# Statistics behind the next maxima, a router's sum one slot later, and an aggregation behind an eviction in a fused attention and routing kernel

## Chip, cores and metric

The kernel runs on one core of one Trainium2 chip. The metric is the device time of one execution in microseconds (us). TensorE multiplies matrices into PSUM, VectorE and ScalarE read PSUM and SBUF, GpSimd reads SBUF, and SyncE issues most of the transfers. In the profile these are PE (with PEld for the loads of weights), DVE, ACT, POOL and SP.

## The reference

The input `x` has 8 batches of 512 rows and 2048 columns. First comes attention in windows of 128 columns with 8 heads, its queries and keys from the normalised `x`, its values from a context. Then each row picks 8 of 64 experts from its normalised logits, is scaled by the sum of their weights and gets a mixture of their biases.

```python
q   = einsum('ed,bdw->bew', Wq, qp) + bq      # qp: patches of layernorm(x)
k   = einsum('ed,bdw->bew', Wk, qp) + bk
val = einsum('ed,bdw->bew', Wv, vp) + bv      # vp: patches of the context
attn = softmax(where(mask > 0, q·k / sqrt(32), -1e9))
o    = gelu(attn · val)
x    = x + tanh(g_xattn) * (Wo·o + bo) * masks
flat   = layernorm(x)                         # over the 2048 columns
scores = softmax(flat @ router_weight.T + router_bias)
topk_w, topk_idx = top_k(scores, 8)
out = x + tanh(g_ffn) * (flat * topk_w.sum() + w_dense @ expert_bias)
```

Two layer norms need the mean and variance of whole rows of 2048 columns: one of `x` ahead of the attention of a batch, one of the attention's result ahead of the batch's routing.

## The kernel before

**Slots.** Each batch is cut into 4 chunks of 512 columns and each chunk into 2 halves of two windows. One half is one slot, g = 0 to 63. A loop runs slots 0 to 61 (8 for a batch, the number called `SPB`); the last two are written out behind it. The order of instructions on every engine is that of the program, by hand; each engine, and SyncE's queue of transfers, takes its instructions strictly in that order.

**A slot on TensorE:** the scores of g (L418) into four PSUM tiles `sc0` to `sc3`, the weighing of values of g-2 (L494), in even slots two output products of chunk ch-2 (`attend`, L524) and in odd ones its logits (L559), the turning of g-1's weights (L472), half of the next chunk's queries and keys (`queries_and_keys`, L356), turnings of the attention's result (`turn_x`, L548), the values of the next chunk's half (L393), and in odd slots two more output products. Values use the tile `sc0`, so the next slot's scores wait until VectorE has evicted the values (`values_out`, L402, tile `vT`). The products of queries and keys, the output products and the logits share two PSUM buffers with the tag `mm` in turn, so each waits for VectorE to read the product before the last. Queries and keys take seven products per half of the features, in four buffers; the fifth product needs the buffer that the sum in L364 reads last.

**A slot on VectorE:** the maxima of g (16 instructions, L437), in even slots two evictions of output products (L530) and the mask (L295), in odd slots the eviction of the logits (L575, L577), the reciprocal of the first sums of exponentials (L457, which needs ScalarE's exponentials, L449), the copies and sums of queries and keys (L363 to L383), the second reciprocal, statistics, the eviction of values, and in odd slots two evictions of output products.

**Statistics of x** come in pieces of 512 columns: 16 for a batch, each loaded (`load_raw`, L91, two buffers) and read by one `bn_stats` (`stats_x`, L245); reading a piece also issues the load of the piece two further on, on SyncE's queue, where it waits for the read. Batch 1 is read in slots 0 to 4, 2, 2, 4, 4 and 4 pieces, later batches two per slot. `stats()` reads the first `PER` = 2 of a slot behind the queries and keys; the call `read_x(len(pieces))` at the slot's end reads what is left, which is two pieces in slots 2, 3 and 4 and none elsewhere. In slot 5 (and every eighth from there) `aggregate` joins the statistics of the next batch.

**Statistics of the result** (`statistics2`, L543) are joined for a batch by `aggregate` in slots with `fin == 2`: slots 10, 18, ... 58. It has four `bn_aggr` on VectorE (L228) and seven small instructions on GpSimd (L230 to L236); their results are read in the next slot by `choose`.

**The router's weights** are centred once: `router_sums` adds them up over the contraction (L772, VectorE), and `centre_router` at the end of slot 3 makes the mean on TensorE (L777) and subtracts it on VectorE (L778). The first logits are those of slot 5.

Of the kernel before, what the change touches and what calls it, by code (L numbers as in the profile page):

```python
# [22 lines left out]
def flamingo_gated_kernel(  # L23
# [34 lines left out]
    NCH = S // CW  # L58
# [35 lines left out]
    def load_xn(ch):  # L94
        t = work.tile([P, NM, CW], F32, tag="xn", name=f"xn_{ch}")
        nc.sync.dma_start(t, rows_of(x, ch // NCH, columns(ch)))
        xn[ch] = t
# [115 lines left out]
    st1, ln1, st2, lns, nmrs = {}, {}, {}, {}, {}  # L213
# [78 lines left out]
    def mask(ch):  # L292

        m01s[ch] = work.tile([P, CW], F32, tag="m01", name=f"m01_{ch}")
        nc.vector.tensor_scalar(m01s[ch], mks[ch], 0.0, scale, ALU.is_gt, ALU.mult)  # L295
# [102 lines left out]
    def values_out(ch, h):  # L398
        pv = pvs.pop((ch, h))
        del cxs[ch, h]  # L400
        vT = work.tile([P, NPP, DK], F32, tag="vT", name=f"vT_{ch}_{h}", bufs=4)
        nc.vector.tensor_tensor(vT, pv, bv_sb[:, None, :].to_broadcast([P, NPP, DK]), ALU.add)  # L402
        vTs[ch, h] = vT
# [74 lines left out]
    def turned(g, k, engine=nc.scalar):  # L478
        p = pairs[g]
        i, e = k // NE, k % NE  # L480
        copy(engine, p["atT"][i][:, e * HR : (e + 1) * HR, :], p.pop("pt"))
# [87 lines left out]
    def logits_out(ch, ms=slice(0, NM)):  # L569
        b = ch // NCH  # L570
        ds = slice(ms.start * P, ms.stop * P)
        pl = pls.pop(ch)[:, ds]
        if ch % NCH == 0:
            lgT[b] = work.tile([P, D], F32, tag="lgT", name=f"lgT_{b}", bufs=1)
            nc.vector.tensor_copy(lgT[b], pl)  # L575
        else:
            nc.vector.tensor_tensor(lgT[b][:, ds], pl, lgT[b][:, ds], ALU.add)  # L577


    experts = {}  # L580
# [190 lines left out]
    def router_sums():  # L771
        nc.vector.tensor_reduce(rwsum, rw_sb.rearrange("p k e -> p e k"), AX.X, ALU.add)  # L772
# [11 lines left out]
    PER = NPIECE // SPB  # L784
    last = NC - 1
    pieces_left = [(b, i) for b in range(1, B) for i in range(NPIECE)]
    for g in range(NG - NH):
        ch, h = g // NH, g % NH
        even = h == 0
        nxt = ch + 1  # L790

        g1 = g - 1 if g >= 1 else None
        g2 = g - 2 if g >= 2 else None

        n_pieces = [2, 2, 4, 4, 4][g] if g < 5 else PER
        pieces = [pieces_left.pop(0) for _ in range(n_pieces) if pieces_left]

        mb, mk = (g - LAG) // SPB, (g - LAG) % SPB
        steps = [mk] if mb >= 0 else []
        xch = ch - 2 if even and ch >= 2 else None  # L800
        lch = ch - 2 if not even and ch >= 2 else None
        pch = ch - 1 if not even and ch >= 1 else None

        vals = [] if (nxt, h) in ((1, 0), (last, NH - 1)) else [(nxt, h)]
        b4 = ch // NCH - 1
        fin = g % SPB if b4 >= 0 else None

        def turn_(k):
            if g1 is not None:
                turn(g1, k)  # L810
                turned(g1, k)

        def turn_x_(k):
            if xch is not None:
                turn_x(xch, k)


        if even:
            if nxt > 1:
                load_cx(nxt, 1)  # L820
            if nxt < last and nxt + 1 >= NCH:
                load_xn(nxt + 1)
        elif nxt < last:
            load_cx(nxt + 1, 0)
        if even and NCH <= ch - 1:
            load_xr(ch - 1)


        scores(g)
        if g2 is not None:  # L830
            weigh(g2)
            weighed(g2)
        maxima(g, (0, 1))
        maxima(g, (2, 3))

        def read_x(n):

            for b, i in pieces[:n]:
                stats_x(b, i)
                if queue:  # L840
                    load_raw(*queue.pop(0))
            del pieces[:n]

        exps(g, 0)
        if even:
            if xch is not None:
                for m in (2, 3):
                    attend(xch, m)
                del os_[xch], mks[xch]
            exps(g, 1)  # L850
            exps(g, 2)
            if g > 0:
                mask(nxt)
            turn_(0)
            turn_(1)
            exps(g, 3)
            if fin != 4:
                for k in steps:
                    scale_x(mb, k)
            if g > 0:  # L860
                divide(g, 0)
            if g == 0:
                load_mask(2)
        else:
            exps(g, 1)
            if lch is not None:
                logits(lch)
                logits_out(lch)
            turn_(0)
            exps(g, 2)  # L870
            exps(g, 3)
            for k in steps:
                scale_x(mb, k)
            if g > 1:
                divide(g, 0)
            b1 = g // SPB + 1
            if g % SPB == 5 and b1 < B:
                ln1[b1] = aggregate(st1.pop(b1), S // 512, f"1_{b1}")
                shares_of_mean(b1)


        def between(i):
            if even:
                if g == 0 and i == 0:
                    divide(g, 0)
                    mask(nxt)
                turn_x_(i)
            elif i == 0:
                if g == 1:
                    divide(g, 0)  # L890
                turn_(1)
                if fin == 3:
                    gather_halves(b4)
                if pch is not None:
                    gelu(pch)
            else:
                turn_(2)
                if pch is not None and nxt < last:
                    load_mask(nxt + 1)

        if even:
            new_queries_and_keys(nxt)
        queries_and_keys(nxt, h, between)
        if not even:
            mask_bias(nxt)
        if fin == 3:
            add_halves(b4)
            choose(b4)
        divide(g, 1)
        if not even and nxt < last:  # L910

            if (nxt + 1) % NCH == 0:
                norm(nxt + 1)
            sums_of_x(nxt + 1, 0)


        if fin == 4:
            select(b4)
        def stats():

            sch = xch if fin != 4 else None
            if fin == 5:
                sch = ch - 2
            if sch is not None:
                for m in range(NM):
                    statistics2(sch, m)
            read_x(PER)

        if fin != 4:
            stats()  # L930
        if fin == 2:
            nmean, rs = aggregate(st2.pop(b4), NCH, f"2_{b4}")
            experts[b4] = {"nmean": nmean, "rs": rs}


        if even:
            turn_x_(2)
            for c_, h_ in vals:
                values(c_, h_, 0, 0)
                turn_(2)  # L940
                values(c_, h_, 1)
            if not vals:
                turn_(2)
            if nxt < last and (nxt + 1) % NCH:
                norm(nxt + 1, (0, 1))
            for c_, h_ in vals:
                values_out(c_, h_)
            if fin == 4:
                stats()
            if fin == 4:  # L950
                turn_weights(b4)
            turn_x_(3)
            turn_(3)
            if nxt < last and (nxt + 1) % NCH:
                norm(nxt + 1, (2, 3))
            if fin == 4:
                for k in steps:
                    scale_x(mb, k)
        else:
            turn_(3)  # L960
            if pch is not None:
                table_of_exps()
            if fin == 3:
                choose_exps(b4)
            for c_, h_ in vals:
                values(c_, h_, 0, 0 if g > 1 else None)
                values(c_, h_, 1)
                values_out(c_, h_)
            if pch is not None:

                for m in (0, 1):
                    attend(pch, m, r=m + 1 if steps else None)
            if nxt < last:
                sums_of_x(nxt + 1, 1)
                sums_of_x(nxt + 1, 2)
        if g == 1:
            nc.scalar.activation(wo_sb, wo_sb, AF.Copy, scale=tgates[:, 0:1])
        if g == 2:
            router_sums()
        if g == 3:  # L980
            centre_router()
        if g == 5:
            load_experts()
        read_x(len(pieces))
        for k in steps:
            mix(mb, k)

# [2 lines left out]
    g = h0 + 1  # L990
# [185 lines left out]
```

## Time and profile before

| | |
|---|---|
| median of three runs | 1316.97 us (1316.94 to 1317.23) |
| the profiled execution's own time | 1316.82 us |
| its span, first to last instruction | 1314.9 us |
| granted TensorE clock, mean | 0.997 |

The stretches from one slot's scores to the next one's, with the busy time of each engine in them (us):

| slot | from, to | length | PE | DVE | ACT | POOL |
|---|---|---|---|---|---|---|
| 2 | 58.00, 72.50 | 14.50 | 14.04 | 10.33 | 10.02 | 10.04 |
| 3 | 72.50, 90.78 | 18.28 | 17.38 | 13.13 | 14.27 | 7.37 |
| 4 | 90.78, 110.41 | 19.63 | 19.09 | 16.58 | 10.63 | 13.18 |
| 5 | 110.41, 130.66 | 20.25 | 19.09 | 12.43 | 15.99 | 9.63 |
| 6 | 130.66, 149.62 | 18.96 | 18.82 | 14.36 | 11.95 | 13.32 |
| 7 | 149.62, 168.43 | 18.81 | 18.81 | 10.96 | 14.48 | 7.25 |
| 10 | 206.21, 225.65 | 19.44 | 18.82 | 14.84 | 12.44 | 13.73 |
| 18 | 364.17, 383.98 | 19.81 | 19.81 | 14.92 | 12.80 | 15.01 |

The granted clock is 1.00 in all of them. From slot 12 on a step of the expert mixture of the batch before is added to each slot (L698 on TensorE, L716 on VectorE). A line of a timeline has the start, the duration, the engine, the line, the operation, the tile written and the tiles read, how many were merged, and in brackets the idle time of the engine before it with what ended it.

### The profile page before, as it was taken

The page shows a single profiled execution, that of the slowest core. Times are in us where ns is not written, and L with a number is a line of the kernel's source. Part 1 is how long each engine was busy: PE and PEld are TensorE (multiplying, and loading weights), DVE is VectorE, ACT ScalarE, POOL GpSimd, SP SyncE. Part 2 cuts the span into 40 slices and gives each one's busy share as a digit, 9 for nine tenths or more (in the row PEclk, how much of TensorE's full clock was granted, in tenths as well). Part 3 has the DMA queues.
Part 4 walks back from the last instruction along what each step waited for, and adds up shares of the span by engine and source line. Part 5 has one row for each costly group of instructions (what it writes and reads, how often), then busy time and mean ns, then how long its engine had stood idle before and what let it go on. Part 6 is the DMA issues. An engine that isn't in the chain of part 4 may idle for free. (4 is left out here: it accounts for less than half of the span.)

```text
span 1314.9 us, 27786 instructions
## 1 busy us (share of the span) xinstructions
PE 1292.9 (98%) x9536; PEld 944.4 (72%) x9536; DVE 925.9 (70%) x3613; ACT 870.1 (66%) x2838; POOL 791.6 (60%) x812
## 2 busy tenths in 40 slices
PE   9999999999999999999999999999999999999996
PEld 6777777777777777777777777777777777777653
DVE  4876767677677776777676786677776776666777
ACT  2776866676765775857667666667656767657652
POOL 3655556675566755577655667556666665575643
PEclk9999999999999999999999999999999999999999
DMA  8333434253444443453443453533544424423224
GB/s 285 97 105 113 114 105 137 97 165 93 152 153 134 149 137 105 152 169 127 155 119 124 153 165 119 167 99 128 169 145 137 153 65 129 138 98 104 73 73 176
DMA packets 109693, 173.40 MB, mean 132 GB/s; under 512 B 9200, under 2 KB 43632, under 8 KB 109424
## 3 DMA queue, kind: packets, MB, share of 16 engines
q1 hardware_dynamic: 107776, 169.27, 40.0%
q10 hardware_dynamic: 1776, 2.36, 0.5%
q8 instruction: 75, 1.23, 0.4%
q14 instruction: 66, 0.54, 0.1%
HBM read 138.06 MB, written 33.55 MB: 131 GB/s over the span
## 5 line engine op out<-in xcount | busy, mean ns | idle before, releaser
L458 POOL TENSOR_TENSOR at<-at,rsum 128x1024 f32<-128x1024 f32 x128 | 244.2, 1908 | 297.5 <-DVE rsum L457 279.8
L449 ACT ACTIVATE at<-at,nmx 128x128 f32<-128x128 f32 x1024 | 396.4, 392 | 4.9 <-DVE nmx L437 4.4
L393 PE MATMUL pv<-wv_sb,cx 128*128 128x256 f32 x1024 | 238.4, 381 | 2.1 <-DMA cx<-in_ctx 2.1
L524 PE MATMUL po<-o,wo_sb 128*128 128x512 f32 x512 | 234.0, 599 | 0.4 <-ACT o L518 0.4
L437 DVE CUSTOM_DVE_ANT_0 at<-sc,m 128x128 f32<-128x128 f32 x1024 | 220.7, 285 | 5.8 <-PE sc L418 5.8
L393 PEld LDWEIGHTS pv<-wv_sb,cx 128*128 128x128 f32 x1024 | 188.5, 191 | 24.7 <-DMA cx<-in_ctx 2.5
L533 POOL TENSOR_TENSOR xr<-t,xr 128x512 f32<-128x512 f32 x124 | 161.4, 1314 | 67.7 <-DVE t L530 67.7
L449 ACT ACTIVATION_READ_ACCUMULATOR at<-at,nmx 128x1 f32 x1024 | 195.0, 190 | 0.0
L476 ACT COPY o<-pa 128x512 f32<-128x512 f32 x63 | 36.9, 585 | 231.2 <-PE pa L494 231.2
L476 ACT COPY atT<-pt 128x512 f32<-128x512 f32 x254 | 140.6, 576 | 52.9 <-PE pt L472 52.7
L524 PEld LDWEIGHTS po<-o,wo_sb 128*128 128x128 f32 x512 | 94.3, 190 | 100.6 <-issue 84.1
L472 PEld LDWEIGHTS pt<-ident,at 128*128 128x128 f32 x1024 | 121.8, 141 | 56.6 <-issue 36.9
L472 PE MATMUL pt<-ident,at 128*128 128x128 f32 x1024 | 150.7, 275 | 0.7 <-ACT atT L476 0.3
L530 DVE SCALAR_TENSOR_TENSOR t<-po,bo_sb,mk 128x512 f32<-128x512 f32 x128 | 95.7, 749 | 62.3 <-PE po L524 62.3
L476 ACT COPY x1T<-px 128x512 f32<-128x512 f32 x120 | 70.2, 586 | 96.0 <-PE px L548 95.9
L356 PE MATMUL qk<-xt,wq_sb 128*128 128x256 f32 x496 | 128.0, 381 | 2.5 <-DVE u L364 2.5
L356 PE MATMUL qk<-xn,wk_sb 128*128 128x256 f32 x496 | 127.8, 380 | 1.6 <-DVE lgT L575 1.2
L356 PE MATMUL qk<-xn,ws 128*128 128x256 f32 x496 | 127.3, 379 | 0.0
L356 PEld LDWEIGHTS qk<-xn,ws 128*128 128x128 f32 x496 | 94.3, 190 | 12.8
L716 DVE TENSOR_TENSOR xr<-pb,xr 128x512 f32<-128x512 f32 x128 | 81.7, 684 | 30.1 <-PE pb L698 30.1
L356 PEld LDWEIGHTS qk<-xn,wk_sb 128*128 128x128 f32 x496 | 89.3, 190 | 11.9 <-DVE lgT L575 1.6
L418 PEld LDWEIGHTS sc<-ks,qs 32*128 32x128 f32 x2048 | 63.2, 186 | 45.8 <-DVE t L530 18.2
(118 smaller groups left out, 2070.3 us busy)
## 6 DMA issues: line engine op xcount, KB each, us to landing
out_dram<-xr SPq DMA_DIRECT2D x63, 512.0 KB, 3.6
cx<-in_ctx SPq DMA_DIRECT2D x62, 512.0 KB, 5.4
raw<-in_x SPq DMA_DIRECT2D x112, 256.0 KB, 3.4
xn<-in_x SPq DMA_DIRECT2D x28, 1024.0 KB, 7.6
xr<-in_x SPq DMA_DIRECT2D x28, 1024.0 KB, 7.5
mk<-in_mask_Bx1x_ff SPq DMA_DIRECT2D x32, 256.0 KB, 5.4
xr<-in_x SPq DMA_DIRECT2D x12, 256.0 KB, 6.3
cx<-in_ctx ACTq DMA_DIRECT2D x2, 512.0 KB, 6.6
```

The source lines that it names most:

```text
L356: nc.tensor.matmul(out_, w_[:, j, es], xb[:, j, :], start=(j == 0), stop=(j == NM // 2 - 1))
L393: nc.tensor.matmul(pv[:, i, :], cx[:, m, i * W : (i + 1) * W], wv_sb[:, m, :], start=(m == 0), stop=(m == NM - 1),)
L418: nc.tensor.matmul(sc[r][:, i, e, :], qss[ch][rows[r], e, ws], kss[ch][rows[r], e, ws], start=True, stop=True,)
L437: nc.vector.tensor_tensor_reduce(p["at"][i][:, e * HR + r, :], p["sc"][r][:, i, e, :], bias, -1.0, BIG, ALU.add, ALU.min, p["nmx"][:, r, i ...
L449: nc.scalar.activation(at, at, AF.Exp, bias=p["nmx"][:, r, i, e : e + 1], scale=-1.0, accum_out=p["rsum"][:, i, h : h + 1],)
L458: (engine or nc.gpsimd).tensor_tensor(p["at"][i], p["at"][i], rs[:, :, None].to_broadcast([P, H, W]), ALU.mult)
L472: nc.tensor.transpose(pt[:, r, :], p["at"][i][:, e * HR + r, :], ident)
L476: (engine.tensor_copy if engine is nc.vector else engine.copy)(out_, in_)
L524: nc.tensor.matmul(po[:, cs], wo_sb[:, e, m * P : (m + 1) * P], os_[ch][:, e, cs], start=(e == 0), stop=(e == NE - 1),)
L530: nc.vector.scalar_tensor_tensor(t[:, cs], po[:, cs], bo_sb[:, m : m + 1], mks[ch][:, cs], ALU.add, ALU.mult)
L533: (engine or nc.gpsimd).tensor_tensor(xc, t[:, cs], xc, ALU.add)
L716: nc.vector.tensor_tensor(xc, pt, xc, ALU.add)
```

## The change

Three moves of instructions within VectorE's order (the first with the loads that it issues on SyncE's queue, the last with the seven instructions on GpSimd); nothing else is changed.

- The pieces that slots 2, 3 and 4 leave over are read in the following slot (3, 4 and 5): in an even slot behind the maxima, the evictions of output products and the mask; in an odd slot behind the maxima and the eviction of the logits. The read at the slot's end is gone.
- `router_sums` goes from the end of slot 2 into slot 3, behind the statistics and ahead of the eviction of values.
- In slots with `fin == 2` the aggregation goes from ahead of the values to behind their eviction.

```diff
@@ -784,6 +784,7 @@
+    pieces = []
     for g in range(NG - NH):
@@ -793,6 +794,7 @@
         n_pieces = [2, 2, 4, 4, 4][g] if g < 5 else PER
+        over = pieces
         pieces = [pieces_left.pop(0) for _ in range(n_pieces) if pieces_left]
@@ -833,7 +835,7 @@
-        def read_x(n):
+        def read_x(n, pieces=pieces):
@@ -851,6 +853,7 @@
             if g > 0:
                 mask(nxt)
+            read_x(len(over), over)
             turn_(0)
@@ -866,6 +869,7 @@
                 logits(lch)
                 logits_out(lch)
+            read_x(len(over), over)
             turn_(0)
@@ -928,9 +932,8 @@
         if fin != 4:
             stats()
-        if fin == 2:
-            nmean, rs = aggregate(st2.pop(b4), NCH, f"2_{b4}")
-            experts[b4] = {"nmean": nmean, "rs": rs}
+        if g == 3:
+            router_sums()
@@ -945,6 +948,9 @@
             for c_, h_ in vals:
                 values_out(c_, h_)
+            if fin == 2:
+                nmean, rs = aggregate(st2.pop(b4), NCH, f"2_{b4}")
+                experts[b4] = {"nmean": nmean, "rs": rs}
             if fin == 4:
@@ -975,13 +981,10 @@
-        if g == 2:
-            router_sums()
         if g == 3:
             centre_router()
         if g == 5:
             load_experts()
-        read_x(len(pieces))
         for k in steps:
```

## The prediction

> **What bounds the kernel.** I read the page's first part, then TensorE's timeline from start to end, then VectorE's and ScalarE's timelines around each hole found there. The page:
>
> ```profile
> span 1314.9 us, 27786 instructions
> ...
> PE 1292.9 (98%) x9536; PEld 944.4 (72%) x9536; DVE 925.9 (70%) x3613; ACT 870.1 (66%) x2838; POOL 791.6 (60%) x812
> ```
>
> TensorE is busy for 98%, so a change of order on VectorE pays only where TensorE stands still for VectorE. The chain of waits covers only the last 15 us and tells nothing here. In TensorE's timeline between 36 and 1230 us seven matmul groups carry an idle time, all before 226 us; the change touches what precedes four of them:
>
> ```profile
> 80.06 1.13 PE L356 MATMUL qk<-xt,wq_sb 128*128 128x256 f32 x4 [0.90 <-DVE u L364]
> ...
> 97.88 1.13 PE L356 MATMUL qk<-xn,wk_sb 128*128 128x256 f32 x4 [0.41 <-DVE t L530]
> ...
> 117.94 1.13 PE L356 MATMUL qk<-xn,wk_sb 128*128 128x256 f32 x4 [1.16 <-DVE lgT L575]
> ...
> 225.65 1.17 PE L418 MATMUL sc<-ks,qs 32*128 32x128 f32 x32 [0.62 <-DVE vT L402]
> ```
>
> They lie in slots 3, 4, 5 and at the end of slot 10. The reader sees a start, a duration, and in brackets how long TensorE waited and for whom. From slot 12 (244.90) to slot 61 (1221.30) the starts of successive scores lie 19.80 to 20.32 us apart in a fixed pattern with no such wait, so a microsecond won before them is kept to the tail.
>
> What VectorE does ahead of those holes:
>
> ```profile
> 72.36 1.95 DVE L772 TENSOR_REDUCE rwsum<-rw_sb 128x64 f32<-128x1024 f32 x1
> 74.24 1.27 DVE L245 BATCH_NORM_STATS2 st<-raw 128x6 f32<-128x512 f32 x2
> 75.43 0.26 DVE L437 CUSTOM_DVE_ANT_0 at<-sc,m 128x128 f32<-128x128 f32 x1
> ...
> 112.61 1.31 DVE L245 BATCH_NORM_STATS2 st<-raw 128x6 f32<-128x512 f32 x2 [2.26 <-DMA raw<-in_x]
> 113.83 0.27 DVE L437 CUSTOM_DVE_ANT_0 at<-sc,m 128x128 f32<-128x128 f32 x1
> ...
> 224.43 0.61 DVE L228 BATCH_NORM_AGGREGATE mv<-st 128x2 f32<-128x24 f32 x4
> 224.96 0.63 DVE L402 TENSOR_TENSOR vT<-pv,bv_sb 128x512 f32<-128x512 f32 x1
> ```
>
> The router's sum and two pieces stand between slot 2's values and slot 3's maxima, two pieces (with a wait for their load) before slot 5's maxima, the aggregation before slot 10's eviction of values. Slot 4 is like slot 5: pieces at 92.52, maxima at 93.71.
>
> **The change, part by part.** No instruction is added or removed; each term is what becomes of one hole.
>
> *Slot 3.* Scores start at 72.50. Where VectorE is free, maxima follow 1.19 us later (slot 2: scores 58.00, maxima 59.19; slot 6: 130.66, 131.85), so at 73.69 instead of 75.43. Sixteen take 3.38 (59.19 to 62.57): end 77.07. The two pieces, moved here, take 1.23: 78.30. Next is the reciprocal, which needs the first eight exponentials. Those stood at 75.80, having waited 0.46 for maxima; they now follow the copy of weighed values (74.75) by 0.48, as in slot 2 (60.25, 60.73): 75.23. In slot 2 the reciprocal came 3.22 after the first exponential (63.95), so 78.45 instead of 79.02. From there VectorE goes on as before, so the sum that TensorE awaits (L364) ends 0.57 earlier and TensorE resumes at 79.49. **Gain 0.57**, no more: ScalarE takes over as the limit. The router's sum now stands before slot 3's eviction: pieces end at 85.57, the sum (1.88 to its successor) at 87.45, the eviction runs to about 88.1 instead of 87.4. Its readers, slot 4's scores, start at 90.21; cover 2.1. The first output addition needs its matmul only at 88.44. Without the cover, up to 0.7 would be lost. The mean over the router's weights needs the sum at about 89.9.
>
> *Slot 4.* TensorE's scores now start at 90.21. Centring of the router's weights runs 90.82 to 91.95; maxima follow at once, to 95.33. The output addition (L530) whose buffer TensorE waits for (97.08 before) runs 95.33 to 96.03. Without the wait the projection starts 0.87 after the two transposes (slot 6: 136.31, 137.18), at 96.73, which is later: the hole goes. It is worth 0.58 at this group (97.88 less 96.43 is 1.45 against 0.87) and 0.11 at the next, which follows a wait by 0.97 instead of 0.86: **0.69**. The pieces then stand behind the mask (97.57 to 98.85), reciprocal to 98.97, copy and sum (L363, L364) to 99.85. The next projection product needs that sum's buffer 3.90 after the projection's start (slot 6: 137.18, 141.08), at 100.63. Cover 0.78.
>
> *Slot 5.* Shifted by 0.57 + 0.69, scores start at 109.15, maxima 110.34 to 113.72, then the logits' eviction to 114.32. TensorE needs it at 115.35 (third product, two steps of 0.86 after the first at 113.63): no hole. **1.33 and 0.11 gone: 1.44.** The pieces end at 115.57, reciprocal and bn_aggr (L228, 0.49) at 116.18, the sum at 117.07; the fifth product needs it at 117.53. Cover 0.46. GpSimd's eight small instructions after the division come to their end about 0.4 later against TensorE; what waits (L378) is needed by nobody for 2 us.
>
> *Slot 10.* The aggregation's four instructions take 0.53 (224.43 to 224.96). Behind the eviction, that starts at 224.43 and the scores 0.74 later, as in slot 6 (148.88, 149.62): 225.17. **Gain 0.48.** The aggregation hides in the 1.25 that VectorE waits for scores. In the six later slots of this kind (18 to 58) it moves into the 0.53 that VectorE waits for the expert mixture (384.08): zero, and at most 0.03 each. GpSimd's seven instructions shift by 0.63 under a wait of 3.00 before the division (390.29): zero.
>
> *Loads.* Each piece read issues the next piece's load, on SyncE's queue. In slots 3 to 5 these loads go behind the context, activation and mask loads, half a slot later; the context's load no longer waits for them. The shortest new interval is slot 3: loads at about 77.7 and 78.3, reads at 84.3, so 6.0 against landings of 3.0 to 9.0, median 3.4. Slot 5's read had waited 2.26 for its load (issued 109.2); now it has 6. The mask load of slot 3 goes from 76.4 to about 79 and is read near 97. I take zero for all; the upper bound is the slower rival.
>
> A check by stage: slot 4 lasts 19.63 and slot 6, with the same matmuls, 18.96; slot 5 lasts 20.25 and slot 7 18.81; slot 10 19.44 and slot 6 18.96: 0.67, 1.44, 0.48.
>
> Sum: 0.57 + 0.69 + 1.44 + 0.48 = **3.18 us**. The profiled execution took 1316.82, so 1313.64; the three runs' median 1316.97 lies 0.15 above it, so 1313.8.
>
> The Trainium skill, "SBUF — State Buffer", section "Who interferes with whom", says that a VectorE operation in a two-port mode, or with two inputs in SBUF, and a GpSimd operation shut each other out for a whole instruction. The mask (L295) bears it out: 0.37 with GpSimd quiet (41.83), 1.06 beside additions (98.40), ending just after the first of them. Four pieces' worth of the same statistics took 2.42 beside a division on GpSimd (106.16), no longer than two took alone (1.23). By that page the moved statistics and the reduction, with one input each, lose nothing; the mask ahead of slot 4's pieces could lose another addition.
>
> **Rivals.**
>
> 1. *The covers in slots 4 and 5 don't hold.* The pieces now stand between maxima and the sum whose buffer TensorE needs. Against: 0.78 and 0.46 left. For: in slot 4 the mask could wait for both GpSimd additions instead of one, 1.28 more, 0.50 beyond the cover; in slot 5 a reciprocal half a microsecond late is enough. Losing 0.5 to 0.6 in each gives about 2.1 gained, 1314.9.
>
> 2. *ScalarE doesn't bind in slot 3.* If the exponentials come 0.6 earlier than I reckon, the hole goes whole: 0.90 + 0.17 + 0.11 = 1.18 instead of 0.57, 1313.2. Against: their predecessor waits on TensorE at 74.75.
>
> 3. *Slower: pieces land late.* Reads now follow their loads behind other transfers; it decides beyond some 6 us of landing. At 9.0, the longest seen, slot 3's pieces (issued near 69.6 and 70.2) are read 1.55 late and cost 1.4 after the reciprocal's slack; its second pair delays the eviction past the scores by 0.5; slot 5's pair ends 2.55 late and costs 2.1. That is 4.0 lost against 3.18 won: 1317.8. Against it: the page's median is 3.4, and 9.0 belongs to the crowded start.
>
> 4. *The time comes back later*, a wait forming at the next slot because ScalarE or GpSimd was only just ready: nearly nothing gained, 1316.5. Against: slots 6 and 7 run the same order without a hole.
>
> **How the numbers follow.** The forecast has 0.66, with 1313.3 to 1314.3 as its own range; rival 1 0.18, rival 2 0.07, rival 3 0.05, rival 4 0.04. A measurement of this kernel can tell 0.2%, 2.63 us, so the border is 1314.34. Almost all of the forecast and rival 2 lie below it: 0.70. Rival 3 counts as slower by half of its weight, with a little for the unforeseen: 0.04. The rest is 0.26. Range 1313.0 to 1315.3: it takes in rivals 1 and 2 and leaves 3 and 4 out.
>
> **What would show it.** Slot 3's scores unmoved at 72.50; the projection there resuming near 79.5 with about 0.3 of wait left on L364; no wait on L530 near 96.7 nor on the logits' eviction near 115.4; slots 4 and 5 lasting 18.9 to 19.0 and 18.8; slot 10 19.0; slots 11 onward unchanged in length. It is wrong if a new bracket on TensorE appears for L364 in slots 4 or 5, for L402 at slot 4's scores, or if VectorE shows a wait for a piece's load.

## The result and the profile after

The changed kernel took 1314.28 us (median of 14 runs, 1314.04 to 1314.38), the kernel before 1316.95 in the same comparison (14 runs, 1316.83 to 1317.23). The ratio is 0.998, with a 95% interval from 0.9972 to 0.9987: 2.67 us less. The interval leaves out 1, and the two sets of runs don't overlap (1314.38 at most after, 1316.83 at least before); the gain is a hair beyond the 2.63 us that the prediction drew as its border. The profiled execution took 1314.31.

The page of the changed kernel, first part:

```profile
span 1312.2 us, 27785 instructions
...
PE 1290.5 (98%) x9536; PEld 942.4 (72%) x9536; DVE 927.1 (71%) x3613; ACT 872.9 (67%) x2838; POOL 792.3 (60%) x812
```

VectorE has the same 3613 busy instructions, and TensorE's share is still 98%. What moved is seen only in TensorE's timeline:

```profile
72.51 1.17 PE L418 MATMUL sc<-ks,qs 32*128 32x128 f32 x32 [0.35 <-DVE vT L402]
79.53 1.13 PE L356 MATMUL qk<-xt,wq_sb 128*128 128x256 f32 x4 [0.36 <-DVE u L364]
...
96.78 1.03 PE L356 MATMUL qk<-xn,wk_sb 128*128 128x256 f32 x4
...
115.41 1.03 PE L356 MATMUL qk<-xn,wk_sb 128*128 128x256 f32 x4
```

Slot 3 starts where it did (72.50 before). Of the 0.90 at the projection 0.36 is left; the 0.41 and 1.16 in slots 4 and 5 are gone, and there the group takes 1.03 instead of 1.13: a group that starts after a wait took 0.1 longer in each of these rows. VectorE's timeline shows why:

```profile
73.70 0.29 DVE L437 CUSTOM_DVE_ANT_0 at<-sc,m 128x128 f32<-128x128 f32 x1 [1.24 <-PE sc L418]
...
77.08 1.28 DVE L245 BATCH_NORM_STATS2 st<-raw 128x6 f32<-128x512 f32 x2
78.48 0.20 DVE L457 RECIPROCAL rsum<-rsum 128x8 f32<-128x8 f32 x1
...
85.53 1.93 DVE L772 TENSOR_REDUCE rwsum<-rw_sb 128x64 f32<-128x1024 f32 x1
87.36 0.69 DVE L402 TENSOR_TENSOR vT<-pv,bv_sb 128x512 f32<-128x512 f32 x1
...
114.38 1.28 DVE L245 BATCH_NORM_STATS2 st<-raw 128x6 f32<-128x512 f32 x2
...
221.80 0.68 DVE L402 TENSOR_TENSOR vT<-pv,bv_sb 128x512 f32<-128x512 f32 x1
222.38 0.62 DVE L228 BATCH_NORM_AGGREGATE mv<-st 128x2 f32<-128x24 f32 x4
```

Slot 3's maxima now wait for TensorE (73.70, not 75.43); the pieces stand behind them, the router's sum ahead of the eviction of slot 3's values. Slot 5's pieces (114.38) carry no wait for their load, which was 2.26. In slot 10 the eviction stands ahead of the aggregation.

The table has the length of a slot, from its first score matmul to the next slot's.

| stretch | before | after | won | forecast |
|---|---|---|---|---|
| slot 3 | 18.28 | 17.74 | 0.54 | 0.57 |
| slot 4 | 19.63 | 18.95 | 0.68 | 0.69 |
| slot 5 | 20.25 | 18.82 | 1.43 | 1.44 |
| slot 10 | 19.44 | 18.95 | 0.49 | 0.48 |
| slots 13 to 60 together | 956.37 | 956.38 | −0.01 | 0 |
| last slot to the end | 64.43 | 64.78 | **−0.35** | 0 |

The windows of the same four slots (length, then busy time and count of each engine, granted clock, DMA share, GB/s) show that TensorE's clock plays no part, and that slots 4, 5 and 10 keep at most 0.14 beyond 18.82 of matmuls:

```profile
72.51:90.25 17.74, 17.38 (x134) 13.54 (x134) 13.18 (x51) 14.22 (x44) 7.38 (x6) 1.00 0.44 124
90.25:109.21 18.96, 18.82 (x150) 14.93 (x149) 16.46 (x56) 10.58 (x41) 13.25 (x11) 1.00 0.31 99
109.21:128.03 18.82, 18.82 (x141) 13.64 (x141) 12.39 (x54) 15.94 (x47) 9.64 (x14) 1.00 0.48 130
203.57:222.53 18.96, 18.82 (x150) 14.92 (x149) 14.41 (x54) 12.00 (x43) 13.31 (x11) 1.00 0.36 132
```

At slot 11's scores TensorE is 3.12 us ahead (225.65 to 222.53). At 1273.00 it is 2.69 ahead. Most of the difference goes in one place, 40 us before the end. First VectorE, then GpSimd, then TensorE of the changed kernel:

```profile
1270.85 0.75 DVE L530 SCALAR_TENSOR_TENSOR t<-po,bo_sb,mk 128x512 f32<-128x512 f32 x1 [2.16 <-PE po L524]
```

```profile
1271.67 1.27 POOL L533 TENSOR_TENSOR xr<-t,xr 128x512 f32<-128x512 f32 x1 [1.64 <-DVE t L530]
```

```profile
1273.00 0.33 PE L548 MATMUL px<-ident,xr 128*128 128x128 f32 x1 [0.42 <-POOL xr L533]
```

and the same addition in the kernel before:

```profile
1273.53 0.75 DVE L530 SCALAR_TENSOR_TENSOR t<-po,bo_sb,mk 128x512 f32<-128x512 f32 x1 [1.81 <-PE po L524]
```

The addition waits for the same matmuls, but idles 2.16 instead of 1.81. The trace's rows of semaphores say more: TensorE's semaphore reached its value at 1270.40 and VectorE's row for the wait is at 1270.43, yet the addition starts at 1270.85, 0.42 later. Before, wait and addition lay 0.07 apart (1273.46 and 1273.53). The late addition makes GpSimd's late, and TensorE's turning waits 0.42 for it. Nothing that the profile shows holds VectorE in between.

### The profile page after: what moved, and what is told of

It is laid out like the page before. It is cut to its first block, busy times and chain, and to the rows that moved or that the text cites. A ratio compares the mean times of both kernels' runs of the same rounds, so it can differ in the third digit from the quotient of the medians.

```text
span 1312.2 us, 27785 instructions
## 1 busy us (share of the span) xinstructions
PE 1290.5 (98%) x9536; PEld 942.4 (72%) x9536; DVE 927.1 (71%) x3613; ACT 872.9 (67%) x2838; POOL 792.3 (60%) x812
## 3 DMA queue, kind: packets, MB, share of 16 engines
q8 instruction: 75, 1.23, 0.4%
## 5 line engine op out<-in xcount | busy, mean ns | idle before, releaser
L449 ACT ACTIVATION_READ_ACCUMULATOR at<-at,nmx 128x1 f32 x1024 | 198.8, 194 | 0.0
L476 ACT COPY o<-pa 128x512 f32<-128x512 f32 x63 | 37.0, 587 | 229.1 <-PE pa L494 229.1
L476 ACT COPY atT<-pt 128x512 f32<-128x512 f32 x254 | 141.2, 579 | 52.7 <-PE pt L472 52.6
L476 ACT COPY x1T<-px 128x512 f32<-128x512 f32 x120 | 70.4, 587 | 94.8 <-PE px L548 94.7
```

The costliest lines, as they stand in the source:

```text
L449: nc.scalar.activation(at, at, AF.Exp, bias=p["nmx"][:, r, i, e : e + 1], scale=-1.0, accum_out=p["rsum"][:, i, h : h + 1],)
L476: (engine.tensor_copy if engine is nc.vector else engine.copy)(out_, in_)
```

## The experiments

**The three parts, one by one.** Theory: the four terms belong to the parts as the prediction has them, with ScalarE as the limit in slot 3, and the 0.35 at the end a matter of VectorE's stream. Rival: parts help or hinder each other. The first four kernels ran on one chip, beside 33 runs of the kernel before with a median of 1316.84.

Pieces alone: the change without these lines, and with the kernel before's in their place.

```diff
-        if g == 3:
-            router_sums()
+        if fin == 2:
+            nmean, rs = aggregate(st2.pop(b4), NCH, f"2_{b4}")
+            experts[b4] = {"nmean": nmean, "rs": rs}
...
-            if fin == 2:
-                nmean, rs = aggregate(st2.pop(b4), NCH, f"2_{b4}")
-                experts[b4] = {"nmean": nmean, "rs": rs}
...
+        if g == 2:
+            router_sums()
```

> Only the pieces move; the router's sum stays at the end of slot 2 and the aggregation ahead of the eviction. Theory (each hole is worth what the later of VectorE and ScalarE leaves of it): in slot 3 maxima start at 74.24 behind the router's sum instead of 73.70, the two pieces end at 78.85, the sum that TensorE awaits ends near 79.9, so TensorE resumes at 79.96, only 0.1 us before the old 80.06. Slots 4 and 5 gain 0.67 and 1.43 as in the changed kernel, slot 10 nothing. Gain up to slot 60: 2.2 us. Rival (each move pays its own time ahead of the maxima): the pieces' 1.19 us is over the hole of 1.07, so slot 3's hole goes whole and the gain is 3.1 us. For the tail: if the 0.37 us that the changed kernel lost after 1249 us belongs to any shifted execution, it is seen here as well and the total is 1.8.

Measured: 1314.50 (11 runs), ratio 0.9981 [0.9973, 0.999], 2.34 less. Slot 3 lasts 18.01 (0.27 won, where some 0.1 was expected), slots 4 and 5 18.95 and 18.82, as in the whole change; slot 10 stays at 19.44 and the end at 64.40. VectorE in slot 3, and TensorE's wait:

```profile
74.21 0.27 DVE L437 CUSTOM_DVE_ANT_0 at<-sc,m 128x128 f32<-128x128 f32 x1
...
77.58 1.27 DVE L245 BATCH_NORM_STATS2 st<-raw 128x6 f32<-128x512 f32 x2
78.78 0.18 DVE L457 RECIPROCAL rsum<-rsum 128x8 f32<-128x8 f32 x1
```

```profile
79.76 1.13 PE L356 MATMUL qk<-xt,wq_sb 128*128 128x256 f32 x4 [0.62 <-DVE u L364]
```

The maxima still stand behind the router's sum (74.21); then VectorE works without a gap to the reciprocal, so here VectorE itself sets the end of the hole.

Router's sum alone, in the kernel before:

```diff
+        if g == 3:
+            router_sums()
...
-        if g == 2:
-            router_sums()
```

> Only the router's sum moves; the pieces stay at the ends of slots 2 to 4. Theory: in slot 3 the pieces stand at 72.4 to 73.6, maxima start at 73.7 when the scores are there, exponentials at 75.25 behind the copy of weighed values, the reciprocal at 78.48, TensorE resumes at 79.53: a gain of 0.53 us, the same as the changed kernel has in slot 3, from this one move alone, and the remaining wait of 0.36 stays because ScalarE sets it. Slots 4, 5 and 10 unchanged. Total 0.5 us. Rival (each move pays its own time): the sum's 1.9 us is over the hole of 1.07, so it goes whole: 1.07 us.

Measured: 1316.62 (11 runs), ratio 0.9997 [0.9988, 1.0006], 0.22 less, within what can't be told from no change; the slots tell more. Slot 3 lasts 17.72, so this part alone wins 0.56 there, as much as the whole change; slots 4 and 10 are as before, and the end lasts 64.79, 0.36 longer. Its reciprocal has a bracket:

```profile
78.58 0.20 DVE L457 RECIPROCAL rsum<-rsum 128x8 f32<-128x8 f32 x1 [0.98 <-ACT at L449]
```

VectorE, done with the pieces ahead of the maxima, stands still for ScalarE's exponentials. With the whole change they fill this gap: the pair at 77.08 and its 1.20 to the successor (77.58 to 78.78 above) make 78.28, and the reciprocal starts at 78.48.

Aggregation alone:

```diff
-        if fin == 2:
-            nmean, rs = aggregate(st2.pop(b4), NCH, f"2_{b4}")
-            experts[b4] = {"nmean": nmean, "rs": rs}
...
                 values_out(c_, h_)
+            if fin == 2:
+                nmean, rs = aggregate(st2.pop(b4), NCH, f"2_{b4}")
+                experts[b4] = {"nmean": nmean, "rs": rs}
```

> Only the aggregation moves behind the eviction. Theory: slot 10 loses the 0.53 us of four small instructions ahead of its eviction and ends 0.48 us earlier; slots 18 to 58 stay as they are; total 0.5 us gain. Rival (the aggregation is exposed behind the eviction in the six later slots, ahead of the expert mixture's additions): up to 0.03 us each in the additions and no effect on TensorE, or, if the next maxima wait for it, 0.5 us lost in each of six slots, 2.5 us slower in all.

Measured: 1316.44 (11 runs), ratio 0.9997 [0.9988, 1.0005], 0.40 less. Slot 10 lasts 18.95 (0.49 won), slots 13 to 60 together 956.38 and the end 64.43 as before; slot 5 came out 0.06 longer and slot 3 0.03, so that 0.40 is left.

The changed kernel once more, as the sum to compare with:

> The changed kernel once more. Theory A (the 0.35 us that VectorE stood with all its semaphores satisfied before an output addition near the end, and which TensorE then waited for, belongs to this program's timing): it is seen again at the same instruction and the gain is 2.7 us. Theory B (it was a chance of that one execution): it is gone, and TensorE keeps 3.05 to 3.12 us to the end of the profiled execution.

Measured: 1314.18 (11 runs), ratio 0.9979 [0.997, 0.9988], 2.66 less. The parts alone make 2.34 + 0.22 + 0.40 = 2.96. The 0.3 between lies in slot 3: 0.27 and 0.56 alone, 0.56 together. The two parts shorten the same hole, and ScalarE allows 0.56. The end is 64.80 again, with the same addition 0.44 behind its wait (1270.32, 1270.76).

**The 0.35 at the end.** The move of the router's sum takes one wait row out of VectorE's stream (3877 rows instead of 3878; 24 maxima with two waits instead of 25), so that every later instruction stands one row earlier. The late addition is row 3775, counted from 0, in each kernel that shows the delay; before, that row was the wait ahead of it. To test it, one instruction of no effect is put at the start of VectorE's stream:

```diff
     nc.vector.memset(half, -0.5)
+    nc.vector.memset(half, -0.5)
```

> The changed kernel with one more instruction on VectorE at the very start (a memset of a small constant, written twice). Theory: moving the router's sum took one wait of its own out of VectorE's stream, so the output addition near the end became VectorE's row 3775 (counted from 0) instead of its wait; a row at 63 beyond a multiple of 128 that must be issued right behind a wait starts 0.35 us late (seen at rows 1087 and 3775 of the changed kernel). One more instruction puts the wait back on row 3775: VectorE's addition follows its wait by 0.07 us, not 0.42, TensorE has no wait for it near 1273 us, and 3.05 to 3.15 us are kept to the end: 0.35 us faster than the changed kernel, about 1313.85. Rival (the stall comes with the earlier timing of the whole program): it stays, and the time is that of the changed kernel.

Measured: 1313.70 (10 runs; before 1316.79 on this chip), ratio 0.9977 [0.9968, 0.9986], 3.09 less. The gain over the kernel before on the same chip was 2.67 and 2.66 without the extra instruction, so one more instruction makes the kernel 0.4 faster:

```profile
1270.27 0.75 DVE L531 SCALAR_TENSOR_TENSOR t<-po,bo_sb,mk 128x512 f32<-128x512 f32 x1 [1.81 <-PE po L525]
```

The idle time is 1.81 again, and the last slot to the end takes 64.42. So the delay hangs on where in VectorE's stream the addition stands, not on what precedes it in time. The expectation's wider claim, that a row 63 beyond a multiple of 128 starts late right behind a wait, fits the traces but rests on two places in the stream. In the changed kernel 51 instructions of VectorE follow a wait row of their own, with the engine idle. Of these 49 start 0.06 to 0.17 after that row and two 0.42 after it, rows 1087 and 3775, the only ones of the 51 that are 63 beyond a multiple of 128. Row 1087 is a copy in slot 18, whose wait row is at 369.51:

```profile
369.93 0.42 DVE L363 COPY s<-qk 128x256 f32<-128x256 f32 x1 [1.70 <-PE qk L356]
```

Its second wait, for GpSimd, was satisfied by 369.26. With the extra instruction the same copy starts 0.07 after its wait row (369.36, 369.43). All kernels that show one of the two delays show both, the others neither; slot 18 lasts 19.81 with or without its one, so that it costs nothing. Row 3007 of the changed kernel is no test: it waited for TensorE until 1012.27, long after its wait row (1011.51), and started at 1012.29.

**Is ScalarE the limit of slot 3?** The reciprocal and the division of slot 3 go behind the fourth product, as slot 1 had it, so that the sum (L364) no longer stands behind a wait for exponentials:

```diff
-            if g > 1:
+            if g > 3:
                 divide(g, 0)
...
-                if g == 1:
+                if g in (1, 3):
                     divide(g, 0)
```

> The changed kernel with slot 3's first reciprocal (and the division that it feeds) behind the fourth product of queries and keys. Theory (ScalarE's exponentials set what is left of slot 3's hole, through the reciprocal that stands ahead of the copies and sums): the remaining 0.36 of wait and what goes with it are gone, slot 3 is 0.5 to 0.65 us shorter (17.1 instead of 17.74), the rest stays, the tail's 0.35 too: about 1313.6. Rival (the two pieces ahead of it set it): they end at 78.3, so the sum would still end near 79.3 and the gain is at most 0.2 us.

Measured: 1313.95 (11 runs), ratio 0.9979 [0.997, 0.9988]; slot 3 lasts 17.65, where some 17.1 was expected. TensorE, then ScalarE:

```profile
79.15 1.13 PE L356 MATMUL qk<-xt,wq_sb 128*128 128x256 f32 x4
...
82.46 0.66 PE L472 MATMUL pt<-ident,at 128*128 128x128 f32 x4
```

```profile
81.84 0.57 ACT L476 COPY atT<-pt 128x512 f32<-128x512 f32 x1
```

The wait for L364 is shorter, not gone. TensorE resumes 0.63 after its transposes (78.52 to 79.15; 0.96 in the changed kernel, 0.43 where nothing waits), too little for a bracket, and the group still takes 1.13. VectorE now works without a gap from the maxima over the two pieces (77.03) to the end of the sum (79.10), so the pieces set what is left of this wait, as the rival has it. The rest of the gain comes back later: the copy of turned weights (L476) stands in ScalarE's order behind all sixteen exponentials of the slot, and the next turning, which needs its buffer, starts 1.04 after the product before it (81.42 to 82.46) instead of 0.87. That ScalarE decides here is shown by the faster version below, whose pieces stand behind the sum too: its slot 3 has no wait for the sum and lasts 17.65 all the same.

```profile
78.19 1.03 PE L357 MATMUL qk<-xt,wq_sb 128*128 128x256 f32 x4
...
81.69 0.66 PE L473 MATMUL pt<-ident,at 128*128 128x128 f32 x4 [0.31 <-ACT atT L477]
```

ScalarE binds, as the prediction has it, but in two places: whoever takes the first away gets 0.07 to 0.09 and not 0.6.

**How much cover is left?** Every piece that a slot leaves over is read twice, which puts some 1.2 more of VectorE's work in each of the slots 3 to 5:

```diff
+        def read_twice():
+            for b, i in over:
+                per = S // SW
+                statistics(b, i // per, i % per, raw[b, i])
+            read_x(len(over), over)
...
-            read_x(len(over), over)
+            read_twice()
```

> The changed kernel with each piece left over read twice, so 1.2 us more of VectorE in the moved place in slots 3, 4 and 5 (the second reading gives the same numbers). Theory (covers as the prediction had them): slot 3 has a cover of 0.1 and loses 1.05; slot 4 has 0.8 to 0.9 and loses 0.3 to 0.5; slot 5 has 0.5 and loses 0.65 to 0.8; the tail's 0.35 is not there because five rows more stand ahead of it. In all 1.8 to 2.1 us over the changed kernel, about 1316.1. Rival (the moved pieces cost nothing wherever VectorE is idle for as long in that slot): no slot is longer.

Measured: 1315.96 (11 runs), ratio 0.9994 [0.9985, 1.0003]. Against the changed kernel slots 3, 4 and 5 are 0.93, 0.48 and 0.76 longer:

```profile
80.44 1.13 PE L356 MATMUL qk<-xt,wq_sb 128*128 128x256 f32 x4 [1.29 <-DVE u L364]
...
101.95 1.13 PE L356 MATMUL qk<-xt,wq_sb 128*128 128x256 f32 x4 [0.21 <-DVE u L364]
...
119.61 1.13 PE L356 MATMUL qk<-xt,wq_sb 128*128 128x256 f32 x4 [0.50 <-DVE u L364]
```

So the same pieces that cost nothing cost what goes beyond the cover, at the very sum that the prediction names; slot 3, with hardly any cover, lost most of the 1.2 (1.05 was expected). Of 1.2 added, slot 4 hid 0.72 and slot 5 0.44 by their lengths, or 0.82 and 0.55 without the 0.1 that a group after a wait takes longer: near the covers of 0.78 and 0.46 that were forecast. The end lasts 64.39, without the delay.

**A faster version.** The extra instruction of the run above stays. Slot 0's pieces are left over to slot 1, the reciprocals and divisions of slots 2 and 3 go behind a later product, and the pieces read in slots 1 and 3 behind those:

```diff
-            if g > 0:
+            if g > 2:
                 divide(g, 0)
...
-            read_x(len(over), over)
+            if g > 3:
+                read_x(len(over), over)
...
-            if g > 1:
+            if g > 3:
                 divide(g, 0)
...
-                if g == 0 and i == 0:
+                if g in (0, 2) and i == 0:
                     divide(g, 0)
...
-                if g == 1:
+                if g in (1, 3):
                     divide(g, 0)
+                    read_x(len(over), over)
...
-            read_x(PER)
+            if g > 0:
+                read_x(PER)
```

> A version to beat both: the changed kernel with the extra row at the start, with slot 0's two pieces read in slot 1, with the pieces of slots 0 and 2 behind the fourth product of the next slot, and with the first reciprocals of slots 2 and 3 there too. Theory: slot 1's wait of 1.09 us for the sum (its maxima stand behind slot 0's pieces) goes nearly whole, 1.2 to 1.35 with what goes with it; slot 2 gains 0.2; slot 3 0.55 to 0.65; the tail 0.35: 2.3 to 2.5 us under the changed kernel, about 1311.8. Rival (slot 1 is bound by ScalarE's exponentials or by the load of the next pieces, which is issued 5 us later): slot 1 gains less than 0.5 and the whole about 1.5.

Measured: 1312.83 (6 runs), ratio 0.997 [0.9958, 0.9981], 3.96 less than before but a microsecond short of what was expected. Slot 1 shows where it went:

```profile
49.48 1.13 PE L357 MATMUL qk<-xt,wq_sb 128*128 128x256 f32 x4
...
53.38 0.66 PE L473 MATMUL pt<-ident,at 128*128 128x128 f32 x4 [0.61 <-ACT atT L477]
```

It is the second place of the run before: the wait for the sum is all but gone (the product starts 0.51 after its transposes, 1.69 before), and 0.61 comes back at the turning. The mend is to let ScalarE copy the turned weights ahead of its last four exponentials in slots 1 and 3:

```diff
-            exps(g, 3)
+            if g > 3:
+                exps(g, 3)
...
                 turn_(1)
+                if g in (1, 3):
+                    exps(g, 3)
```

> The last version with one more step: in slots 1 and 3 ScalarE's last four exponentials of the slot stand behind the copy of the second turned tile instead of ahead of it. Theory (what was left in these slots is ScalarE's order: the fourth turning waits for a buffer that the copy of the second frees, and that copy stood behind all sixteen exponentials): the wait of 0.61 us at slot 1's fourth turning goes, slot 1 lasts 12.9 instead of 13.51, slot 3 about 17.2 instead of 17.65, in all 1.0 us under the last version, about 1311.8. Rival (the division by the second sums, which needs those exponentials, becomes late and the next slot's turnings wait): slots 2 and 4 get longer by what 1 and 3 win.

Measured: **1311.61** (5 runs, 1311.31 to 1311.74) against 1316.86, ratio 0.996 [0.9947, 0.9974], 5.25 less. Slots 1 to 3 last 12.68, 14.27 and 17.12 (before: 14.07, 14.50, 18.28), and slot 4 doesn't lengthen (18.96). Two waits over 0.3 are left on TensorE between 36 and 250 us:

```profile
41.11 1.13 PE L357 MATMUL qk<-xt,wq_sb 128*128 128x256 f32 x4 [0.56 <-DVE u L365]
70.85 1.17 PE L419 MATMUL sc<-ks,qs 32*128 32x128 f32 x32 [0.35 <-DVE vT L403]
```

## Why the prediction was right, point by point

**Reading.** That a change of order on VectorE pays only in TensorE's holes held in the slots of every run: four holes, four terms. The delay at the end lies outside that reading.

**Slot 3**, 0.57 forecast, 0.54 measured. Maxima at 73.70 (73.69 forecast), exponentials 75.25 (75.23), reciprocal 78.48 (78.45), TensorE again at 79.53 (79.49). That ScalarE takes over as the limit is shown by the router's sum alone, whose reciprocal waits 0.98 for exponentials. The later reciprocal brings the sum 0.38 forward (end at 79.10 instead of 79.48), and then the pieces are the limit there. What the prediction didn't see is that the pieces' move adds nothing here: the router's sum alone buys all of it.

**Slots 4 and 5**, 0.69 and 1.44 forecast, 0.68 and 1.43 measured, from the pieces alone in their run. The working's times held to 0.1: the sum (L364) ends at 99.80 in slot 4 (99.85 forecast) and at 116.99 in slot 5 (117.07). The product that needs the sum's buffer starts at 100.67 and 117.58, which leaves 0.87 and 0.59 of cover, some 0.1 more than forecast. What waits for GpSimd in slot 5 (L378) waits 1.58 instead of 1.18, and nobody waits for it, as forecast.

**Slot 10**, 0.48 forecast, 0.49 measured; zero at the later slots, as said.

**Loads**, forecast at nothing. From 60 to 130 us pieces land in 3.0 to 5.3 us, median 3.4, and no read waits.

**Statistics beside GpSimd.** The Trainium skill, "SBUF — State Buffer", section "Who interferes with whom", lets a VectorE operation with one input in SBUF, outside the two-port modes, run undisturbed beside GpSimd. Here the router's sum took 1.93 beside two of GpSimd's operations (84.61 to 87.73) against 1.95 in its old place, and slot 4's pair 1.27 beside GpSimd's two additions (96.19 to 98.88): the trace agrees. (The prediction's 2.42 for four pieces is to be held against twice the 1.23 of two.)

**The sum.** The terms make 3.18; the slots gave 3.14 (0.54 + 0.68 + 1.43 + 0.49). The step that was off is "a microsecond won before them is kept to the tail". Slot lengths were kept up to slot 60, but the tail gave 0.35 back, through VectorE's late addition. The time came out at 1314.28 and not 1313.8, inside the forecast's own range (up to 1314.3) by a hair, and the gain at the border that it drew. That is luck: nothing in the working sized the 0.35. Without the delay (the run with one more instruction) the gain is 3.09, the forecast's 3.18 within 0.1.

**The rivals.** The covers hold (rival 1): reading twice is what their failing looks like, with brackets that the changed kernel lacks. ScalarE does bind (rival 2): 0.36 of wait is left. Pieces don't land late (rival 3). Time coming back later (rival 4) happened for 0.35 of 3.12, not at the next slot and not by an engine that was only just ready.

## What to carry to other kernels

Where one engine is busy for 98%, list its holes; work moved off the way to a hole is worth at most that hole, taken by the spacing of the groups (a bracket of 1.16 stood for 1.43 here), and less where a second engine stands right behind: forecast that engine's own earliest time before adding parts up, since two parts that shorten one hole don't add. A stage of the same kind without the hole is the best check of such a sum, and here it gave each term to 0.03. After taking one wait away, follow the same engine's order to the next buffer it frees: in slots 1 and 3 the best version needed the late reciprocal and pieces on VectorE and the early copy on ScalarE.

## What the hardware showed that was not expected

An instruction of VectorE started 0.42 us after its wait was satisfied and nothing in the profile held it (wait row 1270.43, start 1270.85). It was seen, with 0.42 to 0.44, in the three kernels in which that instruction is row 3775 of VectorE's stream (the changed one in both of its profiles, the router's sum alone, the later reciprocal), and in none of the others, where wait and start lie 0.06 to 0.07 apart; one more instruction of no effect, 1270 us earlier, removed it and 0.4 us of the kernel's time. The same four profiles show the same delay at row 1087, 21 times 128 rows earlier.

A cause in how instructions reach the engine would fit a delay bound to a place in the stream: the Trainium skill, "Runtime: NRT & Kernel Launch", section "Instruction fetch mechanics", says that instructions are refilled in blocks of 256 while the engine runs and that crossing into a new block is mostly hidden. The trace shows such refills, in smaller blocks. The changed kernel's page has a queue of kind "instruction":

```profile
q14 instruction: 66, 0.54, 0.1%
```

Its packets hold 8 KB each. The rows of VectorE, ScalarE, GpSimd and SyncE together are 8564, which makes 130 rows for a packet. Of these 66 packets, 23 come while VectorE stands at a row 56 to 65 beyond a multiple of 128, where 5 would if they were spread evenly. One comes at 1271.51, as row 3776 starts, 0.66 behind the start of the late addition. In the kernel before, one comes at 1271.67, while VectorE waits for TensorE, 1.86 ahead of the addition. So the late instruction stands about where VectorE passes from one block of instructions to the next, and where a wait stands there instead, the passage falls into the wait. That the passage itself takes the 0.42 is not shown: no row times it, and at row 1087 the nearest packet lies 2.2 away. What is shown is the size: on a change worth 3.1 us, a shift by one row gave back 0.35, a ninth.
